# Layer 3: six of eight retrieved tiles turned in 32x32 squares and by transfers within SBUF, not by TensorE

## The chip, the cores and the metric

One core of a Trainium2 chip runs the whole program. The metric is device time in microseconds (us) of one execution, the median over several runs. All data is float32 unless a tile says otherwise.

## The reference

Four layers follow each other on x, which has 4 x 256 tokens of 512 features. Each layer normalises x and adds an attention part and a feed-forward part. Only the attention of layer 3 is touched here. It looks values up in a compressed memory:

```
q   = xn @ Wq.T + bq            # 8 heads of 128 (one per group of 4)
sig = elu(q) + 1
num = sig @ M[h]                # per head, 128 x 128
den = sig @ z[h] + 1e-6
retrieved = num / den           # per head, tokens x 128
out = repeat(retrieved, 4 heads) @ Wo.T
```

Since each retrieved head is used for four heads of Wo, the kernel adds up those four blocks of Wo beforehand, so `out` is a product with 8 x 128 = 1024 rows of summed output weights.

## The kernel before

The tokens are eight tiles of 128. A half is four of them. Large products are done in blocks by a seven-product scheme (Strassen's in Winograd's form, `seven`, L1325), so a product needs sums of input blocks as well as the blocks: s1 = a21 + a22, s2 = s1 - a11, s3 = a11 - a21, s4 = a12 - s2 (`summed`, L1105). Each of the seven products is a task.

The instructions of TensorE, VectorE, ScalarE and GpSimd are issued in the order in which the program writes them (`manual_schedule`, L1286). SyncE issues the transfers. Work is placed with `run(tasks)`, `after(k, f)` and `spread(k, steps)`: `after` puts f behind the task that comes k tasks later. Each engine works through its own list in that order and waits at an instruction whose inputs or buffer aren't ready.

The output of TensorE goes to eight PSUM banks with one buffer each (tags S, U, T, V, X, Y, Z, W). A bank must be read out by VectorE or ScalarE before TensorE can use it again.

Around the change, tile t = 0 to 7 goes through these steps:

- `retrieved(t)`, L1728: sixteen matmuls in three banks S, U, V (`num`, L1736, 129 columns per head, the last one the denominator). Then VectorE makes `den` (L1750) and its reciprocal (L1752), and ScalarE scales the eight heads into `ret` in SBUF (L1758, eight instructions). `ret` has three buffers.
- `turned(t, j, tag)`, L1765: four heads at a time, j = 0 and 1, are transposed by TensorE with the identity (`retT`, L1770, four instructions) into bank T (or Y) and copied by VectorE into a quarter of the half's input blocks (`rt_a`, L1776). Features must lie on the partitions, as the next product sums over them.
- `turned_sums(half)`, L1778: the four block sums on VectorE, 128 x 1024 elements each (`rt_s`, L1111, and L1115).
- `output_tasks` of the half: seven products of sixteen matmuls each with the summed weights (`wos_b`, `wos_t`; L1413).

Tiles 0 to 3 are half 0. Their steps are laid between the fourteen products of the second half's queries (L1377): `num` of tile t stands behind the (2t + 1)th of them, the two turnings behind the next two. Between those products VectorE also reads out query banks (`u`, `c`, `m` at L1349, L1357, L1367) and makes elu(q) + 1 from `e` and `sig` (L1694, L1700). The sums of half 0 are spread behind the tenth to thirteenth of the fourteen. Tiles 4 to 7 are half 1 and are laid between the output products of half 0, the sums of half 1 behind its last one. Then the output products of half 1 end the program.

Layer 2 has a step of the same kind as the change. It turns its probabilities in 32 x 32 squares on VectorE (L1853, `blocks<-p`) and moves the squares to their partitions by four transfers (L1858, `q<-blocks`).

Of the kernel before, what the change touches and what calls it, by code (L numbers as in the profile page):

```python
# [21 lines left out]
F32 = mybir.dt.float32  # L22
# [4 lines left out]
AF = mybir.ActivationFunctionType  # L27
ALU = mybir.AluOpType
# [3 lines left out]
P = 128  # L32
B, T, C = 4, 256, 512
# [18 lines left out]
L3_HEADS, L3_G = 8, 4  # L52
# [4 lines left out]
def block_stack(ctx: ExitStack, tc: tile.TileContext, d: dict, out: bass.AP):  # L57
    nc = tc.nc
# [13 lines left out]
    def ps(tag, shape, name):  # L72
        return banks["pool"].tile(shape, F32, tag=tag, name=name, bufs=banks["tags"][tag])
# [34 lines left out]
    for t in range(2):  # L108
# [3 lines left out]
    ident = const.tile([P, P], F32, name="ident")  # L112
# [7 lines left out]
        out=by_four,  # L120
        in_=by_four,
# [1141 lines left out]
    def layers_2_and_3(w, late):  # L1263
# [8 lines left out]
        with ExitStack() as stack:  # L1272
# [36 lines left out]
            A = w.A  # L1309
# [11 lines left out]
            def after(k, *fs):  # L1321

                due.setdefault(slot[0] + k, []).extend(fs)
# [199 lines left out]
            class Layer3:  # L1523
# [204 lines left out]
                def retrieved(self, t):  # L1728

                    half, i, tt = t // 4, t % 4 // 2, t % 2  # L1730
                    banks = []
                    for tag, h0, n in (("S", 0, 3), ("U", 3, 3), ("V", 6, 2)):
                        b = ps(tag, [P, n, ME], f"num_{t}_{h0}")
                        for k in range(n):
                            j, s, e = (h0 + k) // 4, (h0 + k) % 4 // 2, (h0 + k) % 2
                            nc.tensor.matmul(  # L1736
                                b[:, k, :],
                                lhsT=self.sig[half, s, (i, j)][:, e, tt * P : (tt + 1) * P],
                                rhs=self.mz[:, h0 + k, :],
                                start=True,  # L1740
                                stop=True,
                            )
                        banks.append((b, n))
                    ret = self.rets[t] = []

                    def divided():
                        den = small.tile([P, L3_HEADS], F32, tag="den", name=f"den_{t}")
                        for b, n in banks:
                            h = slice(len(ret), len(ret) + n)
                            nc.vector.tensor_scalar(den[:, h], b[:, :, P], 1e-6, None, ALU.add)  # L1750
                            ret.extend([None] * n)
                        nc.vector.reciprocal(den, den)  # L1752
                        r = self.late.tile([P, L3_HEADS, P], F32, tag="ret", name=f"ret_{t}", bufs=3)
                        h = 0
                        for b, n in banks:
                            for k in range(n):
                                ret[h] = r[:, h, :]
                                nc.scalar.activation(  # L1758
                                    ret[h], b[:, k, 0:P], AF.Copy, scale=den[:, h : h + 1]
                                )  # L1760
                                h += 1

                    after(0, divided)

                def turned(self, t, j, tag):  # L1765
                    half, i, tt = t // 4, t % 4 // 2, t % 2
                    A = self.retrieval[half]
                    tp = ps(tag, [P, 4, P], f"retT_{t}_{j}")
                    for k in range(4):
                        nc.tensor.transpose(tp[:, k, :], self.rets[t][4 * j + k], ident)  # L1770
                    key = f"a{i + 1}{j + 1}"
                    if key not in A:
                        A[key] = self.rt[half].tile(
                            [P, 4, T], F32, tag="rt", name=f"rt_{half}_{key}", bufs=7
                        )
                    nc.vector.tensor_copy(A[key][:, :, tt * P : (tt + 1) * P], tp)  # L1776

                def turned_sums(self, half):  # L1778
                    def make(k):
# [266 lines left out]
            l3 = Layer3()  # L2046
            for quad in range(QUADS - 1):
                gp, r = divmod(quad, 4)
# [22 lines left out]
                else:  # L2071
# [15 lines left out]
                    elif quad % 2 == 0 and quad < QUADS - 2:  # L2087

                        k = quad // 2
# [48 lines left out]
            for t in range(4):  # L2138
                k = len(tasks) + 2 * t
                after(k, lambda t=t: l3.retrieved(t))  # L2140
                for j in range(2):
                    after(k + 1 + j, lambda t=t, j=j: l3.turned(t, j, "T"))
            spread(len(tasks) + 9, l3.turned_sums(0))
            spread(len(tasks) + 6, [lambda t=t: l3.biased(t) for t in range(NT)])
            tasks += l3.query_tasks(1, 0) + l3.query_tasks(1, 1)
# [4 lines left out]
            for i, t in enumerate(range(4, NT)):  # L2150
                after(2 + i, lambda t=t: after(0, lambda: l3.retrieved(t)))
                for j in range(2):
                    after(3 + i, lambda t=t, j=j: l3.turned(t, j, "TY"[j]))
            after(6, lambda: [f() for f in l3.turned_sums(1)])
            run(tasks)
            run(output_tasks(l3.retrieval[1], l3.outputs, 1, fresh=True, last=True))
# [107 lines left out]
def _arrays(i):  # L2264
    c, j, r = np.meshgrid(np.arange(4), np.arange(8), np.arange(16), indexing="ij")
    order0 = (P * c + 8 * r + j).reshape(4, P)
    a = dict(_constants())
    a["x"] = i["L0_attn_x"].reshape(B * T, C)
    for n in ("wq", "wk", "wv"):
        a[n] = _chunked(i["L0_attn_" + n].T, order0)  # L2270
    a["wo"] = _chunked(i["L0_attn_wo"].T)

    def padded(w, axis, n):

        shape = list(w.shape)
        shape[axis] = n - shape[axis]
        return np.concatenate([w, np.zeros(shape, w.dtype)], axis)


    scales, zeros = [], []  # L2280
    for m in ("gate", "up"):
        q = padded(i[f"L0_ffn_{m}_qweight"], 1, NBLK * P).reshape(4, 16, NBLK, 16, 8)
        a[m + "_q"] = q.transpose(1, 2, 0, 4, 3).reshape(16, NBLK, 4, P)
        s = padded(i[f"L0_ffn_{m}_scales"], 1, NBLK * P).reshape(4, NBLK, 16, 8)
        scales.append(s.transpose(3, 2, 1, 0).reshape(P, NBLK, 4))
        zeros.append(padded(i[f"L0_ffn_{m}_zeros"], 1, ROWS).reshape(4 * NBLK, 16))
    a["gu_s"] = np.stack(scales, 1)
    a["gu_z"] = np.concatenate(zeros)
    q = padded(i["L0_ffn_down_qweight"], 0, ROWS).reshape(NBLK, 16, C)
    a["down_q"] = q.transpose(1, 0, 2)  # L2290
    a["down_s"] = i["L0_ffn_down_scales"]
    a["down_z"] = i["L0_ffn_down_zeros"]

    a["w1"] = _chunked(i["L1_ffn_W"].T)
    a["rank"] = _chunked(np.concatenate([i["L1_ffn_A"], i["L1_ffn_gate_w"]]).T)
    a["b1_rank"] = i["L1_ffn_B"].T
    a["b1_bias"] = i["L1_ffn_b"][None]
    a["gate_b"] = i["L1_ffn_gate_b"]
    a["bqk"] = np.stack([i["L1_attn_bv_q"].T, i["L1_attn_bv_k"].T], 1)
    a["bv"] = i["L1_attn_bv_v"]  # L2300

    wqkv = i["L2_attn_Wqkv"].T.reshape(2, 2, P, 48, P)
    nq = L2_GROUPS * L2_QH
    q = wqkv[:, :, :, :nq].reshape(2, 2, P, 4, 2, 2, 2, P)
    q = q.transpose(3, 5, 0, 4, 2, 1, 6, 7)
    kv = wqkv[:, :, :, nq:].reshape(2, 2, P, 2, 4, 2, P)
    kv = kv.transpose(4, 0, 5, 2, 1, 3, 6)
    a["wq2"] = q.reshape(8, 4, P, 2, 2 * P)  # L2310
    a["wkv2"] = kv.reshape(4, 4, P, 2, 2 * P)
    wo = i["L2_attn_Wo"].T.reshape(4, 2, 2, 2, P, 2, 2 * P)
    a["wo2"] = wo.transpose(0, 2, 1, 5, 4, 3, 6).reshape(8, 4, P, 2, 2 * P)
    w2 = i["L2_ffn_W_base"].T.reshape(2, 2, P, 2, 2 * P)
    a["w2"] = w2.transpose(0, 3, 2, 1, 4).reshape(1, 4, P, 2, 2 * P)
    ar = np.concatenate([i["L2_ffn_A_w"], i["L2_ffn_router_w"]]).T
    a["ar"] = _chunked(np.pad(ar, ((0, 0), (0, 32 - ar.shape[1]))))
    a["cores"] = i["L2_ffn_cores"].reshape(EXPERTS * RANK, RANK).T
    a["bw"] = i["L2_ffn_B_w"].T
    a["b2"] = i["L2_ffn_b_base"]  # L2320

    m, k, q = np.meshgrid(np.arange(2), np.arange(2), np.arange(P), indexing="ij")
    order3 = (2 * P * m + 2 * q + k).reshape(NC, P)
    wq3 = i["L3_attn_Wq"].reshape(L3_HEADS, L3_G, P, C)[:, 0].reshape(L3_HEADS * P, C)
    w = wq3.T[order3.reshape(-1)].reshape(2, 2, P, 2, 2, 2, P)
    a["wq3"] = w.transpose(4, 0, 3, 2, 1, 5, 6).reshape(2, 4, P, 2, 2 * P)
    a["bq3"] = i["L3_attn_bq"].reshape(L3_HEADS, L3_G, P)[:, 0].T
    a["wo3"] = i["L3_attn_Wo"].T.reshape(L3_HEADS, L3_G, P, C).transpose(0, 2, 1, 3)
    a["mz"] = np.concatenate([i["L3_attn_M"], i["L3_attn_z"][:, :, None]], -1).transpose(1, 0, 2)
    a["pk3"] = _chunked(i["L3_ffn_weight_packed"].reshape(C, C // 2).T)  # L2330
    a["scale3"] = i["L3_ffn_scale"][:, 0]
    a["zero3"] = i["L3_ffn_zero_point"][:, 0]
    a["b3"] = i["L3_ffn_bias"]
    return {k: np.ascontiguousarray(v) for k, v in a.items()}
# [17 lines left out]
```

## Time and profile before

| | us |
|---|---|
| median of three runs (1354.12 to 1357.17) | 1356.17 |
| the profiled execution | 1355.85 |
| its span on the core | 1354.1 |
| TensorE busy | 1306.8 |
| VectorE busy | 930.0 |
| layer 3 from its first `num` to the end of the span | 1253.3 to 1354.1 |

The profiled execution took 1.75 us more than its span. Times in a trace are us from the start of the span. The granted TensorE clock was 0.995 of full speed over the run. A matmul's recorded end is modelled and lies behind the start of the next one, so for TensorE the distance from start to start counts, which is what the chain of waits shows.

### The profile page before, as it was taken

The numbers are of one execution on the slowest core, as the hardware profiler recorded it, in microseconds if no ns is written. First come the engines' busy times: TensorE is split into PE (matmuls) and PEld (weight loads), VectorE is DVE, ScalarE is ACT, GpSimd is POOL, SyncE is SP. The second block draws the span as 40 slices with busy tenths as digits, with TensorE's granted clock in tenths as the row PEclk, the third lists the DMA queues.
The fourth block names the chain that finished last, engine by engine and source line by source line (L and its number), as shares of the span: only waits on it lengthen the run. The fifth ranks groups of instructions, "written<-read, shape, count | busy, mean of one in ns | idle before, by whom it ended". The sixth has DMA issues, their size and how long they took to land. (4 is left out here: it accounts for less than half of the span.)

```text
span 1354.1 us, 20458 instructions
## 1 busy us (share of the span) xinstructions
PE 1306.8 (97%) x7076; PEld 1024.0 (76%) x7076; DVE 930.0 (69%) x1969; ACT 561.7 (41%) x1474; POOL 658.1 (49%) x662
## 2 busy tenths in 40 slices
PE   9899999899998998999999999999999999899998
PEld 7566666588545667888888888888888888677887
DVE  7676667478927249846867968777678776668654
ACT  2444434388212213423443443444434454555530
POOL 4555456477746104663576745757356563021410
PEclk9999999999999999999999999999999999999999
DMA  5022222400610021331333424433334333413001
GB/s 203 14 48 43 41 48 68 101 1 0 175 66 8 0 85 40 83 82 51 113 114 94 124 63 122 116 94 101 81 87 125 90 78 83 144 24 117 1 1 62
DMA packets 92792, 101.44 MB, mean 75 GB/s; under 512 B 21147, under 2 KB 65846, under 8 KB 92305
## 3 DMA queue, kind: packets, MB, share of 16 engines
q1 hardware_dynamic: 91760, 99.08, 26.4%
q8 instruction: 56, 0.92, 0.3%
q10 hardware_dynamic: 816, 0.79, 0.2%
q14 instruction: 48, 0.39, 0.1%
q0 software_dynamic: 112, 0.26, 0.1%
HBM read 67.02 MB, written 7.91 MB: 55 GB/s over the span
## 5 line engine op out<-in xcount | busy, mean ns | idle before, releaser
L1830 ACT ACTIVATE p<-p,nm 128x256 f32<-128x256 f32 (+1 forms) x256 | 113.2, 443 | 158.1 <-DVE nm L1814 157.3
L1427 POOL TENSOR_TENSOR q<-q,t 128x512 f32<-128x512 f32 x64 | 82.0, 1281 | 130.1 <-DVE t L1432 128.3
L1845 ACT ACTIVATE p<-p,rs 128x256 f32<-128x256 f32 (+1 forms) x256 | 95.5, 444 | 39.9 <-DVE rs L1841 39.9
L1377 PE MATMUL m<-xT,wq_b 128*128 128x256 f32 x448 | 103.9, 380 | 2.1 <-ACT kv L1483 2.0
L1432 DVE TENSOR_TENSOR t<-m,rope_sb 64x512 f32<-64x512 f32 (+1 forms) x144 | 95.3, 662 | 1.9
L1377 PEld LDWEIGHTS m<-xT,wq_b 128*128 128x128 f32 x448 | 82.4, 190 | 12.7 <-ACT kv L1483 2.4
L1360 POOL TENSOR_TENSOR c<-c,z 128x512 f32<-128x512 f32 x28 | 36.5, 1303 | 112.8 <-DVE c L1357 54.5
L1853 DVE STREAM_TRANSPOSE blocks<-p 128x768 f32<-128x768 f32 x64 | 62.6, 978 | 41.1 <-ACT p L1845 39.4
L1413 PE MATMUL m<-wo_b,o 128*128 128x256 f32 x384 | 89.6, 379 | 0.0
L1881 ACT COPY o<-av 128x512 f32<-128x512 f32 x64 | 37.3, 583 | 118.2 <-PE av L1871 115.8
L1814 DVE CUSTOM_DVE_ANT_0 p<-s,cmask 128x256 f32<-128x256 f32 (+1 forms) x256 | 76.1, 353 | 12.9 <-PE s L1795 11.2
L475 POOL TENSOR_SCALAR_AFFINE_SELECT keys<-keys 128x256 f32<-128x256 f32 x128 | 56.7, 453 | 49.9 <-ACT keys L471 43.6
L1492 DVE TENSOR_TENSOR x_sb<-x_sb,m 128x512 f32<-128x512 f32 x82 | 54.9, 679 | 36.6 <-PE m L1413 25.3
L1413 PEld LDWEIGHTS m<-wo_b,o 128*128 128x128 f32 x384 | 71.9, 190 | 9.2
L757 PE MATMUL dn<-wd,hT 128*128 128x512 f32 x176 | 76.4, 593 | 0.7 <-ACT o L753 0.7
L814 POOL TENSOR_TENSOR sa<-sa,sb 128x1024 f32<-128x1024 f32 x22 | 62.2, 2830 | 30.6 <-DVE sb L809 30.6
L1377 PE MATMUL m<-x_s,wq_t 128*128 128x256 f32 x320 | 74.1, 380 | 2.4 <-ACT kv L1483 2.0
L471 ACT ACTIVATE keys<-st 128x384 f32<-128x384 f32 x128 | 55.9, 487 | 38.9 <-PE st L461 38.9
L1870 PE MATMUL av<-q,kv 128*128 128x512 f32 x128 | 66.5, 601 | 3.9 <-DMA q<-blocks 3.9
L1377 PEld LDWEIGHTS m<-x_s,wq_t 128*128 128x128 f32 x320 | 60.2, 190 | 12.1 <-ACT kv L1483 2.4
L1795 PE MATMUL s<-kv,q 128*128 128x256 f32 x256 | 65.9, 380 | 0.4 <-POOL q L1427 0.4
L757 PEld LDWEIGHTS dn<-wd,hT 128*128 128x128 f32 x176 | 33.2, 190 | 41.1 <-issue 39.5
(328 smaller groups left out, 3283.8 us busy)
## 6 DMA issues: line engine op xcount, KB each, us to landing
q<-blocks SPq DMA_DIRECT2D x256, 96.0 KB, 2.3
wq_b<-in_wq SPq DMA_DIRECT2D x38, 256.0 KB, 2.8
wo_b<-in_wo SPq DMA_DIRECT2D x32, 256.0 KB, 2.8
raw<-in_wo SPq DMA_DIRECT2D x24, 256.0 KB, 3.2
wkv_b<-in_wkv SPq DMA_DIRECT2D x16, 256.0 KB, 2.8
wos_d<-wos_row SPq DMA_DIRECT2D x28, 128.0 KB, 3.3
gate_q<-in_gate_q SPq DMA_DIRECT2D x11, 256.0 KB
up_q<-in_up_q SPq DMA_DIRECT2D x11, 256.0 KB
```

The costliest lines, as they stand in the source:

```text
L757: nc.tensor.matmul(po, lhsT=hT[:, k, t * P : (t + 1) * P], rhs=wd[:, k, :], start=k == 0, stop=k == NBLK - 1,)
L814: nc.gpsimd.tensor_tensor(self.a, self.a, self.b, ALU.add)
L1377: nc.tensor.matmul(out[:, i, :], lhsT=b[:, c, i * P : (i + 1) * P], rhs=a[:, c, :], start=start and i == 0 and c == 0, stop=i == 1 and c == 1,
L1413: nc.tensor.matmul(out[:, t, :], lhsT=a[:, c, t * P : (t + 1) * P], rhs=b[:, c, :], start=start and t == 0 and c == 0, stop=t == 1 and c = ...
L1427: after(1 + 2 * pause, lambda: nc.gpsimd.tensor_tensor(dst, dst, t2, ALU.add))
L1432: nc.vector.tensor_tensor(t2[at], src[of], sin[of], ALU.mult)
L1795: nc.tensor.matmul(s1[:, i, :], lhsT=q[:, i, P:T], rhs=kt[:, 0, :], start=True, stop=True)
L1814: nc.vector.tensor_tensor_reduce(out=x[f"p{part}"][:, e, :], in0=x[f"s{part}"][:, e, :], in1=cmask if part else cmask[:, P : 2 * P], scale ...
L1830: nc.scalar.activation(p, p, AF.Exp, bias=x["nm"][:, part, e : e + 1], scale=-1.0, accum_out=x["sums"][:, part, e : e + 1],)
L1845: nc.scalar.activation(p, p, AF.Copy, scale=x["rs"][:, part, e : e + 1])
L1853: nc.vector.transpose(blocks, x["p"].rearrange("p e x (b i) -> p b (e x) i", b=4))
L1870: nc.tensor.matmul(av, lhsT=v[:, 0:P], rhs=q[:, :, :, 0:64], start=True, stop=False)
```

## The change

For tiles 0 to 5, TensorE no longer transposes. VectorE turns the four heads of a `turned` step in one instruction, in 32 x 32 squares, from `ret` into a tile `blocks` in SBUF that has two buffers, so that the turning of tile t + 1 waits until the transfers of the same j of tile t have landed. Then SyncE issues four transfers, one for each group of 32 partitions, that move the squares from SBUF to SBUF into the quarter `A[key]`. A transfer is 64 KB, from 32 partitions to 128, in pieces of 32 elements, which is 128 B. The PSUM copy (`rt_a`) falls away with the transposes.

By this path feature 32 b + i comes to lie on partition 4 i + b, where TensorE's transpose leaves feature f on partition f. So the weights Wo are laid out in the same order on the host (`wo3`), and for tiles 6 and 7, which TensorE still turns, ScalarE writes `ret` in that order. `ret` has two buffers instead of three.

```diff
-                        r = self.late.tile([P, L3_HEADS, P], F32, tag="ret", name=f"ret_{t}", bufs=3)
+                        r = self.late.tile([P, L3_HEADS, P], F32, tag="ret", name=f"ret_{t}", bufs=2)
+                        self.rets[t] = r
...
-                                ret[h] = r[:, h, :]
-                                nc.scalar.activation(
-                                    ret[h], b[:, k, 0:P], AF.Copy, scale=den[:, h : h + 1]
-                                )
+                                dst, src = r[:, h, :], b[:, k, 0:P]
+                                if t >= 6:
+                                    dst = dst.rearrange("p (i b) -> p b i", b=4)
+                                    src = src.rearrange("p (b i) -> p b i", b=4)
+                                nc.scalar.activation(dst, src, AF.Copy, scale=den[:, h : h + 1])
...
-                def turned(self, t, j, tag):
+                def turned(self, t, j):
                     half, i, tt = t // 4, t % 4 // 2, t % 2
                     A = self.retrieval[half]
-                    tp = ps(tag, [P, 4, P], f"retT_{t}_{j}")
-                    for k in range(4):
-                        nc.tensor.transpose(tp[:, k, :], self.rets[t][4 * j + k], ident)
+                    ret = self.rets[t][:, 4 * j : 4 * j + 4, :]
...
-                    nc.vector.tensor_copy(A[key][:, :, tt * P : (tt + 1) * P], tp)
+                    if t >= 6:
+                        tp = ps("TY"[j], [P, 4, P], f"retT_{t}_{j}")
+                        for k in range(4):
+                            nc.tensor.transpose(tp[:, k, :], ret[:, k, :], ident)
+                        nc.vector.tensor_copy(A[key][:, :, tt * P : (tt + 1) * P], tp)
+                        return
+                    b = self.late.tile([P, 4, 4, 32], F32, tag="blocks", name=f"blocks_{t}_{j}", bufs=2)
+                    nc.vector.transpose(b, ret.rearrange("p k (b i) -> p b k i", b=4))
+                    for a in range(4):
+                        n = tt * P + 32 * a
+                        nc.sync.dma_start(out=A[key][:, :, n : n + 32], in_=b[32 * a : 32 * a + 32])
...
-    a["wo3"] = i["L3_attn_Wo"].T.reshape(L3_HEADS, L3_G, P, C).transpose(0, 2, 1, 3)
+    wo3 = i["L3_attn_Wo"].T.reshape(L3_HEADS, L3_G, 4, 32, C)
+    a["wo3"] = wo3.transpose(0, 3, 2, 1, 4).reshape(L3_HEADS, P, L3_G, C)
```

TensorE's list loses twelve groups of four transposes, SyncE's gains twelve groups of four transfers, and VectorE's keeps its order and length, with a turning in squares wherever a copy out of PSUM stood. The stores of the output come behind the new transfers on SyncE, in the order of before.

## The prediction

> **What bounds the kernel now.** TensorE is busy for 1306.8 of 1354.1 us, so a gain must come out of TensorE's list or its waits. The chain of waits for the stage, cut where it repeats, shows which engine ends last:
>
> ```profile
> 1271.25 0.44 PE retT L1770 x4
> 1271.69 1.73 PE m L1377 x8
> 1273.42 0.44 PE retT L1770 x4
> 1273.86 1.79 PE num L1736 x16
> 1275.64 1.73 PE m L1377 x8
> 1277.37 0.45 PE retT L1770 x4
> ...
> 1281.03 0.67 DVE e L1694 x2
> 1281.70 1.13 DVE rt_s L1111
> 1282.83 1.20 DVE sig L1700 x2
> ...
> 1287.84 0.61 DVE c L1357
> 1288.45 0.04 issue
> 1288.50 1.99 PE m L1377 x8
> ```
>
> From 1258 to 1278 TensorE is the chain, and a group of four transposes costs 0.44 us of it. From then to 1288.5 VectorE is. Busy times by stage (columns: stretch, length, then PE, PEld, DVE, ACT, POOL busy, clock, DMA share, GB/s) say the same, and that no transfers run here:
>
> ```profile
> 1266.00:1272.00 6.00, 6.00 (x42) 5.49 (x41) 2.44 (x8) 2.54 (x10) 2.80 (x3) 1.00 0.00 1
> ...
> 1278.00:1290.00 12.00, 10.92 (x51) 8.77 (x50) 12.00 (x17) 6.15 (x15) 2.69 (x3) 1.00 0.00 0
> ...
> 1300.00:1326.00 26.00, 26.00 (x167) 23.76 (x167) 11.06 (x31) 9.18 (x33) 0.00 (x0) 1.00 0.01 2
> ```
>
> VectorE has 12.00 of 12.00 us to do while half 0's sums are made. Whatever delays the first sum (s1, 1281.62 in the timeline) delays TensorE at 1288.50 one for one.
>
> The price of the new path is read from the same step in layer 2, from the view of its tile `blocks`:
>
> ```profile
> L1858 SPq DMA_DIRECT2D q<-blocks x256: 542/602/1510, 543.1 to 1205.2; - x128
> L1853 DVE STREAM_TRANSPOSE blocks<-p x64: 966/978/980, 542.1 to 1202.3; 128x768 f32<-128x768 f32 x64
> ...
> DMA to landing us min/median/max: 2.3/2.3/4.4
> ```
>
> In SyncE's timeline, four of these issues take 2.59 us, 0.65 each.
>
> **Removed.** Tiles 0 to 3: eight groups x 0.44 = 3.5 us of TensorE, and the 1.40 us that it waits at 1258.35 for the first `ret`. Tiles 4 and 5: two pieces of the chain, 0.87 and 1.14, so 2.0 us, in a stretch where TensorE is never idle. Taken alone that is 6.9 us. The PSUM copies stood off the chain but for the last.
>
> **Added on VectorE.** Twelve turnings of 128x512. At 978 ns for 768 columns one is between 0.65 (in proportion) and 0.98 us; the copy that it replaces took 0.69. I take 0.70, so nothing. What changes is what it waits for: four `ret` instructions (0.27 us each) and, from tile 1 on, the landing of the four transfers of the tile before. Behind it on VectorE stand `den`, without which no `ret` comes, and the bank readings `u`, `c`, `m`, for which TensorE waits.
>
> **Added on SyncE.** 48 issues. Tiles 0 to 3 have 32 of them, 32 x 0.65 = 20.8 us, one after the other from about 1259.8. The nearest other row in spacing is two 512-piece transfers (`gate_z`, `up_z`), issued at 64.45 and 64.96, 0.51 us apart. Bounds 0.51 and 0.65; I take 0.65, since `q<-blocks` also goes from 32 partitions to 128. Nothing is queued behind these transfers but the output stores, first issued at 1331.93.
>
> **Added on the DMA engines.** A transfer is 64 KB in 512 pieces of 128 B. No row has such pieces. The nearest are 512 pieces of 256 B (`up_z`, 128 KB) and 128 of 768 B (`q<-blocks`, 96 KB), in two stretches that hold little else:
>
> ```profile
> 88.00:88.40 0.40, 0.40 (x16) 0.13 (x4) 0.40 (x2) 0.28 (x1) 0.40 (x1) 1.00 0.98 184
> ...
> 544.40:546.90 2.50, 2.50 (x17) 2.32 (x16) 2.37 (x5) 0.00 (x0) 2.32 (x2) 1.00 0.69 148
> ```
>
> By count of pieces a transfer occupies the engines as long as `up_z` does: 128 KB / 184 GB/s = 0.71 us. By bytes at 148 GB/s it is 0.44. Both lie near the 0.65 between issues, so I let the issue set the pace; the upper end I put at 1.0 us, since the 512 pieces of `gate_z`, beside a 256 KB transfer, ended only after the 2.1 us from 80.0 to 82.1. Landing: `q<-blocks` has 2.3 us, the low end; `gate_z`, as many pieces, has 4.3 at least, the high end, but behind that 256 KB transfer, which at 184 GB/s is 1.4 us of it. I take 4.3 - 1.4 = 2.9, the row with as many pieces.
>
> Here a rule speaks against the change. The Trainium skill, DMA: Bandwidth & Descriptors, Specifications, gives 512 B as the least transfer for line rate, smaller ones being read, modified and written. Taken so that a 128 B piece costs what a 512 B one does, it makes an estimate of 1.8 us a transfer and some 37 us on the sum. The same page, Why small descriptors are slow (HBM only), exempts transfers from SBUF to SBUF, which would leave 0.44 us and this forecast. The 256 B pieces above ran at 184 GB/s at a share of 0.98, the 768 B ones at 148 / 0.69 = 214, which is nearer to the second; no run here shows 128 B.
>
> **The sum.** With spacing 0.65 and landing 2.9, step by step (B = turning, D = last of its four transfers landed):
>
> - Tile 0: `ret` begins at 1257.93 as now, its fourth ends 1259.0. B00 1259.1 to 1259.8; four issues from 1259.8, the last at 1261.75, D00 1264.65. B01 1260.4 to 1261.1, issues from 1262.4, D01 1267.25.
> - Tile 1: without transposes `num` ends at 1260.95 instead of 1263.24, `ret` begins at 1262.3 instead of 1263.94. But B10 waits for D00, to 1265.4, and B11 for D01, to 1268.0. D10 1270.25, D11 1272.85.
> - Tile 2: `c` 1268.0, `den` 1268.6, `ret` 1269.2 (now 1270.05). B20 to 1271.05, B21 waits for D11, to 1273.6. D20 1275.9, D21 1278.5.
> - Tile 3: `m`, `e`, `den`, `ret` 1275.25 (now 1276.25). B30 to 1277.1, B31 to 1279.25. Issues for B30 from 1277.1, for B31 from 1279.7, D31 1284.55.
>
> So TensorE is up to 4 us ahead at tile 2, and VectorE takes it back: s1 needs tile 3's transfers and begins at 1284.6 instead of 1281.62. Before, its input came by a PSUM copy that ended 0.6 us earlier; now VectorE stands idle from about 1279.9 to 1284.6. The 6.8 us of VectorE from s1 to TensorE's wait at 1288.50 have no gap to make it up, so 3.0 us are lost there, in place of the 4.9 us gained.
>
> In the last stage 1.8 of the 2.0 us remain: tile 4's transfers land about 1313 and tile 5's by 1321 before the shift, while TensorE reads that quarter first at 1325.4; 0.2 is for `ret` of tile 6, whose `den` now stands behind two turnings. Tiles 6 and 7 with their strided `ret`: nothing (a copy of that kind, `o<-av`, takes 583 ns for 512 columns against 590 for plain ones).
>
> Sum: +3.0 - 1.8 = +1.2 us. On the profiled 1355.85 that is 1357.05, on the median 1356.17 it is 1357.4. About 0.2% (2.7 us) is what a measurement of this kernel tells from no change, so this is no change that can be told. Landing 2.3 instead of 2.9 gives s1 at 1283.1, so -0.3; the count-bound pace of 0.71 gives s1 at about 1286.2 and +3 us. This case alone holds -0.5 to +3: 1355.7 to 1359.2.
>
> **Rivals.**
>
> 1. *The transfers land late, slower.* The ring of two ties tile t + 1 to tile t. If landing is 4.0, a tile lasts 0.7 + 3 x 0.65 + 4.0 = 6.65 us against TensorE's 5.25 (2 x 1.73 + 1.79): s1 at 1288, +6.5, of which the last stage gives back 1.5, so +5. It decides from a landing of about 3.3 us on. For it: four times the pieces. Against: 2.3 is steady over 256 transfers.
> 2. *The engines set the pace, slower by more.* At 1.0 us a transfer the 32 take 32 us, s1 begins near 1259.8 + 32 + 1.9 = 1293.7, +12. It begins above 0.71 us. For it: a source of 32 partitions and the smallest pieces yet. Against: 0.44 by bytes.
> 3. *SyncE issues faster, faster kernel.* With 0.51 and 2.3 the same list gives D00 1263.6, D11 1270.3, D21 1275.35, D31 1280.5: s1 1.1 us earlier than now, -1.1 - 1.8 = -2.9. For it: 0.51 between transfers of as many pieces. Against: 0.65 wherever 32 partitions go to 128.
>
> **How the numbers follow.** Forecast case 0.40, of which 0.32 within 0.2% and 0.08 slower; rival 1 0.26; rival 2 0.12; rival 3 with anything better 0.22. So faster 0.22, same 0.32, slower 0.46: the likeliest single case lies within 0.2%, though the slower ones together hold more. The range runs from 1352.9 (rival 3 and 0.4 below) to 1368.0 (rival 2 at 1.0 us).
>
> **What would show it.** Right: SyncE issues 0.65 us apart without pause in the stage, B10, B11 and B21 idle before a DMA, and VectorE idle for 4 to 5 us before the first `rt_s`, at 1284 to 1285. Wrong: spacing under 0.55 or landings over 3.3, `rt_s` before 1282 or after 1287, or TensorE waiting between the output products of half 0 (1290 to 1326), where I see no new wait.

## The result and the profile after

| kernel | median, us | lowest to highest | runs |
|---|---|---|---|
| before | 1354.35 | 1350.39 to 1357.17 | 12 |
| after | 1358.01 | 1356.05 to 1360.73 | 12 |

The ratio after to before is 1.0030, with a 95% interval from 1.0018 to 1.0042. So the change makes the kernel slower by some 4 us. The median lies within the predicted range and 0.6 us above the predicted time. Part of that nearness is owed to the kernel before, whose median was 1.8 us lower here than in the three runs that the prediction started from: the difference is +3.7 us where +1.2 was forecast. The measured 0.30% lies outside the likeliest case, within 0.2%, though the lower end of the interval, 0.18%, touches it.

The profiled execution of after took 1356.17 us with a span of 1354.5, hardly more than that of before. Its work ahead of the change happened to run 3.9 us earlier: the first `den` of tile 0 is at 1253.39 in its timeline and at 1257.31 in that of before. All that the change touches lies behind this instruction, so below every time is counted from the first `den`.

| from the first `den`, us | before | after | difference |
|---|---|---|---|
| first sum (s1, `rt_s`) | 24.31 | 28.31 | +4.00 |
| first output product of half 0 | 33.02 | 38.17 | +5.15 |
| first output product of half 1 | 68.11 | 72.34 | +4.23 |
| end of the span (known to 0.1) | 96.8 | 101.1 | +4.3 |

The loss arises before half 0's output products, and a piece of it comes back in the last stage. The chain of waits of after shows where (start us, us, what):

```profile
1270.32 1.02 DVE e L1694
...
1273.06 0.71 DVE blocks L1784
1273.77 0.84 DVE sig L1700
...
1275.98 0.70 DVE blocks L1784
...
1277.36 1.02 SPq L1787
...
1279.10 2.43 DMA rt_a<-blocks
...
1281.70 1.23 DVE rt_s L1111
...
1286.32 5.41 PE m L1377 x16
...
1317.80 1.97 PE retT L1780 x8
```

Where `retT` and products carried the chain before, it now goes through VectorE's `e`, `sig` and turnings, SyncE's queue (SPq) and the landing of the last transfer to s1. From there it goes on through VectorE to TensorE's products at 1286.32. The windows of after, with the columns of before:

```profile
1266.00:1272.00 6.00, 6.00 (x36) 5.17 (x34) 3.43 (x8) 2.81 (x10) 6.00 (x6) 1.00 0.66 90
1272.00:1278.00 6.00, 2.38 (x9) 2.03 (x9) 4.26 (x6) 5.48 (x17) 2.90 (x3) 0.90 0.59 81
1278.00:1290.00 12.00, 8.45 (x27) 6.66 (x27) 8.30 (x11) 2.30 (x5) 1.32 (x1) 0.78 0.17 22
```

VectorE, busy for all 12.00 us of the third window before (and for 11.30 us of 1281.92 to 1293.92, the stretch that lies as far behind the first `den`), now works 8.30 of them. TensorE is busy for 2.38 of the 6 us from 1272, and the granted clock falls to 0.90 and 0.78, where it was 1.00 before. The view of the tile `blocks` prices the new path:

```profile
L1787 SPq DMA_DIRECT2D rt_a<-blocks x48: 609/634/1342, 1255.9 to 1317.4; - x48
L1784 DVE STREAM_TRANSPOSE blocks<-ret x12: 695/711/712, 1255.2 to 1314.5; 128x512 f32<-128x512 f32 x12
...
  DMA rt_a<-blocks: 9.1, 5
...
  DVE rt_s L1111: 4.4, 1
```

and the DMA view of after from 1253 to 1284 gives the landing of half 0's 32 transfers, in the median:

```profile
rt_a<-blocks SPq DMA_DIRECT2D x32, 64.0 KB, 2.5
```

VectorE waited 9.1 us for transfers ahead of five turnings and 4.4 us ahead of s1. In the trace the issues stand mostly 0.68 us apart, and the usual landing, from the start of an issue, is 2.45 us.

The clock is a new item. TensorE's timeline of after (in brackets: idle time before, and what ended it):

```profile
1275.63 2.71 PE L1377 MATMUL m<-x_s,wq_t 128*128 128x256 f32 x8 [3.62 <-ACT sig L1688]
...
1286.32 3.14 PE L1377 MATMUL m<-x_s,wq_b 128*128 128x256 f32 x8 [3.55 <-ACT z L1352]
1289.25 2.48 PE L1377 MATMUL m<-xT,wq_t 128*128 128x256 f32 x8
```

Eight such products stand 1.73 us from start to start at full clock. From 1286.32 they take 2.93 and then 2.31 us (1291.56, the first output product, less 1289.25). The trace's clock records have half speed for 3.41 us from 1276.77 and again from 1287.01, each behind an idle time of over 3.5 us. Before, no half speed is recorded between 1253 and 1350.

### The profile page after: what moved, and what is told of

The parts are those of the page before. It is cut to its first block, busy times and chain, and to the rows that moved or that the text cites. A ratio compares the mean times of both kernels' runs of the same rounds, so it can differ in the third digit from the quotient of the medians.

```text
span 1354.5 us, 20478 instructions
## 1 busy us (share of the span) xinstructions
PE 1303.2 (96%) x7028; PEld 1023.0 (76%) x7028; DVE 931.0 (69%) x1969; ACT 561.8 (41%) x1474; POOL 657.2 (49%) x662
```

## The experiments

The theory: half 0's sums stand in VectorE's fixed order, and the new path brings their input about 4 us too late. The late transfers also let TensorE fall idle, which costs clock. The rivals: the loss comes from the last stage, from the ring of two buffers alone, from the DMA engines, or from the clock alone. Each run was also timed against the kernel before; "ratio" is against that. Times are from the first `den`, in us.

| run | s1 | first output product | end of span | ratio (95% interval) |
|---|---|---|---|---|
| before | 24.31 | 33.02 | 96.8 | 1 |
| after | 28.31 | 38.17 | 101.1 | 1.0030 (1.0018 to 1.0042) |
| e1_tail_only | 24.42 | 33.13 | 95.4 | 0.9988 (0.9976 to 1.0000) |
| e2_head_only | 28.56 | 39.54 | 103.5 | 1.0043 (1.0029 to 1.0058) |
| e3_late_sums | 29.30 | 33.60 | 96.4 | 0.9985 (0.9970 to 1.0000) |
| e8_before_late_sums | 29.22 | 32.07 | 95.9 | 0.9995 (0.9983 to 1.0006) |
| e9_tail_late | 31.03 | 33.88 | 96.1 | 0.9989 (0.9977 to 1.0000) |
| e5_four_blocks | 27.42 | 38.18 | 100.0 | 1.0016 (1.0002 to 1.0029) |
| e6_two_queues | 27.47 | 36.19 | 98.0 | 1.0017 (1.0004 to 1.0030) |
| e12_both | 27.41 | 36.12 | 97.9 | 1.0019 (1.0006 to 1.0032) |
| e7_filled | 27.78 | 38.61 | 102.2 | 1.0031 (1.0017 to 1.0046) |
| e11_filled_half | 27.86 | 37.78 | 100.0 | 1.0011 (0.9997 to 1.0024) |
| e13_pool_later | 27.65 | 38.76 | 101.0 | 1.0042 (1.0026 to 1.0059) |
| e10_two_queues_late | 30.01 | 32.85 | 95.1 | 0.9981 (0.9969 to 0.9993) |

An interval is some 3 us wide. The times tell the slow group (1.003 to 1.004) from the fast one (0.998 to 1.000). The intervals of the middle group (1.001 to 1.002) overlap that of after, so there, and within a group, only the traces can tell, and they are of one execution each.

### The two halves of the change (e1_tail_only, e2_head_only)

In the first, only tiles 4 and 5 go the new way, in the second only tiles 0 to 3; the other tiles use TensorE as before.

```diff
-                                if t >= 6:
+                                if t not in (4, 5):
...
-                    if t >= 6:
-                        tp = ps("TY"[j], [P, 4, P], f"retT_{t}_{j}")
+                    if t not in (4, 5):
+                        tp = ps("T" if t < 4 else "TY"[j], [P, 4, P], f"retT_{t}_{j}")
```

> Only tiles 4 and 5 are turned by VectorE and moved by transfers; tiles 0 to 3, 6 and 7 by TensorE. Queue theory (the loss of the changed kernel lies in half 0, where 32 transfers pass one queue before the first block sum): half 0 is as before, s1 starts as long after the first den as before (24.3 us), no half-speed clock in the stage, and the last stage keeps what four transpose groups cost: 0.9 to 2.0 us less than the kernel before. Rival (small transfers cost wherever they stand, VectorE's waits eat the gain): no gain or a loss, 0 to +2 us.

> Only tiles 0 to 3 by the new path, tiles 4 to 7 by TensorE. Queue theory: the whole loss of half 0 without the gain of the last stage: s1 about 28.3 us after the first den (24.3 before), the half-speed clock as in the changed kernel, +5 us on the kernel before, 1 to 2 us above the changed kernel. Rival (the loss is spread over both halves): +2 to +3 us.

Measured: 0.9988 and 1.0043. The two effects, -0.12% and +0.43%, add up to the +0.30% of the change, rounding aside. So the last stage gains about 1.5 us, though the interval of e1 reaches to 1.0000, and half 0 loses nearly 6. With tiles 0 to 3 on TensorE, s1 is back at 24.42.

### Half 0's sums later (e3_late_sums, e8_before_late_sums)

The same edit in after (e3) and in before (e8):

```diff
-            spread(len(tasks) + 9, l3.turned_sums(0))
+            spread(len(tasks) + 12, l3.turned_sums(0))
```

> The changed kernel with the four block sums of half 0 placed three tasks later (spread behind tasks 14 to 17 after the second half's queries begin, not 10 to 13). In-order theory (VectorE stands 4.4 us at the first sum for the last landing, with query readings behind it): that wait falls under 1 us, the output products begin 4 to 5 us earlier than in the changed kernel, 3 to 5 us less in all, so 0 to 1.5 us below the kernel before. Rival (the transfers' ring holds VectorE back anyway, at the turnings): the wait only moves, less than 1.5 us regained.

> The kernel before with its block sums of half 0 placed three tasks later, the control for the other run. If VectorE's full stretch from 1278 to 1290 is what TensorE waits for there (0.25 + 1.19 + 0.68 us), it gains 1 to 2 us on the kernel before. If the sums then delay the output products, it gains nothing.

Measured: 0.9985 and 0.9995, so the edit takes 0.45% (6 us by the times, 4.7 us by the traces) off the change and hardly anything off the kernel before. VectorE's timeline of e3:

```profile
1279.74 0.69 DVE L1784 STREAM_TRANSPOSE blocks<-ret 128x512 f32<-128x512 f32 x1
...
1286.49 1.22 DVE L1111 TENSOR_TENSOR rt_s<-rt_a,rt_a 128x1024 f32<-128x1024 f32 x1
```

Between the two VectorE makes the query work that was queued behind s1, and s1 waits for nothing (no bracket). The last transfer lands 28.2 us after `den`, later than the 28.1 of after; yet the output products begin at 33.60, not 38.17. So what cost time was not that the transfers were late, but that an instruction waiting for them stood in VectorE's order ahead of work that TensorE needed. This is the clearest of the runs.

### Tail alone with later sums (e9_tail_late)

e1_tail_only with the edit of e3.

> VectorE and transfers for tiles 4 and 5 alone, TensorE for tiles 0 to 3 and 6 and 7, and half 0's sums three places later. Theory (the last stage's gain of 1.4 to 1.6 us is there for the taking and the later sums cost nothing): 1.5 to 3 us faster than the kernel before, the best so far. Rival (the later sums push half 0's output products back without the early turning): as the kernel before, within 1 us.

Measured: 0.9989, 1.5 us faster, the lower edge of what was expected, and no better than e1_tail_only without the edit. The rival, within 1 us of before, lies inside the interval too. The trace can't decide, for it has 3.41 us of half speed from 1255.74, where no other trace has any: TensorE's eight products at 1255.52 last 3.19 us there instead of 1.73, and s1 and the first output product, at 31.03 and 33.88, each come 1.81 us later than in e8.

### Four buffers (e5_four_blocks)

The squares of j = 1 go into another pool's two buffers, so each j has a ring of its own.

```diff
-                    b = self.late.tile([P, 4, 4, 32], F32, tag="blocks", name=f"blocks_{t}_{j}", bufs=2)
+                    if j:
+                        b = lnp.tile([P, C], F32, tag="xn", name=f"blocks_{t}_{j}")
+                        b = b.rearrange("p (b k i) -> p b k i", b=4, k=4)
+                    else:
+                        b = self.late.tile([P, 4, 4, 32], F32, tag="blocks", name=f"blocks_{t}_{j}", bufs=2)
```

> The change with a ring of two buffers for each j, so four for the turned squares instead of two. Theory (the sums stand in order behind 32 issues of 0.68 us): the 9.1 us of VectorE's waits for transfers go, but the queue stays: 24 issues are through 18.9 us after the first den, tile 3's values come about then, and 8 more issues and a landing of 2.4 us put the first sum at 26.9 instead of 28.3; with what the freed VectorE brings the gates forward 1.5 to 2.5 us of the 4.3 are regained. Rival A (the two-buffer ring is the whole cost): all 4 us come back, the first sum at 24.3. Rival B (neither the ring nor the queue, only the landing of the last transfer): nothing, within 0.5 us of the change.

Measured: 1.0016, s1 at 27.42. From the view of its tile `blocks`, waits ahead of turnings and ahead of s1:

```profile
  DMA rt_a<-blocks: 1.3, 1
...
  DVE rt_s L1111: 7.7, 1
```

Of the 9.1 us of waits ahead of turnings 1.3 remain, and the wait ahead of s1 grows from 4.4 to 7.7. The 32 issues now stand without a pause from 2.53 to 24.82 us after `den`, and the last lands at 27.24. So with the ring out of the way the queue alone keeps s1 at 27.4: that part of the theory holds, and the ring is worth 0.9 us of s1. The longer stop of VectorE left TensorE idle for 8.10 us, with half clock for 10.24, so the first output product came no earlier than in after. What the trace regains by its end, 1.1 us, comes from the last stage, which the theory did not name: no turning of tile 5 waits for a transfer there, and tile 6's transposes take their old 0.87 us in the chain instead of 1.97.

```profile
1316.90 0.87 PE retT L1780 x8
```

### Two queues (e6_two_queues, e12_both)

e6 is after with half of the issues on ScalarE's queue, e12 the same with the four buffers of e5.

```diff
-                        nc.sync.dma_start(out=A[key][:, :, n : n + 32], in_=b[32 * a : 32 * a + 32])
+                        (nc.scalar if a > 1 else nc.sync).dma_start(out=A[key][:, :, n : n + 32], in_=b[32 * a : 32 * a + 32])
```

> The change with the third and fourth transfer of each group issued by ScalarE instead of SyncE. Theory (the issues set the pace): a group passes in 1.4 us instead of 2.7, the last lands about 24 us after the first den, the first sum runs on time at 24.3, and 3 to 5 us come back. Rival A (the 16 DMA engines set the pace, busy 0.70 now): landing stretches over 3.5 us and under 1 us comes back. Rival B (ScalarE pays): its 16 issues of some 0.6 us delay ret and sig, the gates come late, and at most 2 us come back.

> e5_four_blocks and e6_two_queues together: four buffers, and half of the transfers issued by ScalarE. Theory (once the ring no longer holds the turnings and the queue has half the issues, nothing else is late): the last transfer lands before 24.3 us after the first den, the first sum runs on time, VectorE waits for no transfer, and 3 to 4 us of the 4.3 come back. Rival (16 issues take ScalarE 10 us, which ret and sig wait for): the first sum at 26 to 27.5 as in e5_four_blocks and e6_two_queues alone, and under 2.5 us come back.

Measured: 1.0017 and 1.0019, with s1 at 27.47 and 27.41. My theory falls in both: halving the queue did not bring s1 to 24.3. The signs of both rivals of e6 are there. From the view of e12's tile `blocks`, who waited for a turning:

```profile
  ACT ret L1761: 3.3, 1
  ACT acc L1502: 2.6, 1
  ACT u L1347: 1.5, 1
```

ScalarE works in order too: its issues wait for the turning and then take about 0.68 us each (median of 24: 675 ns), and `u`, `ret` and, in the last stage, `acc` stand behind them. Tile 3's first turning begins 18.56 us after `den` in e12, and 15.91 in e5. That is rival B. With two issues at a time the landings grew too, in the median to 3.9 us (SyncE) and 3.4 (ScalarE) in e6, and the last, of 4.31 us, is what s1 waits for. While both queues issued, the DMA engines were busy for 0.97 of the time at 138 GB/s (e12, 1264 to 1267), where one queue had kept them busy for 0.71. That is rival A: a second queue meets the limit of the engines. How much each rival took was not separated. Still both traces show the output products 2 us earlier than after. Only 0.84 us of that is s1 in e6, and the rest is the clock. In e6's TensorE timeline:

```profile
1286.22 1.99 PE L1377 MATMUL m<-x_s,wq_b 128*128 128x256 f32 x8 [1.85 <-ACT z L1352]
1288.49 1.99 PE L1377 MATMUL m<-xT,wq_t 128*128 128x256 f32 x8 [0.28 <-DVE c L1357]
1290.33 3.62 PE L1413 MATMUL m<-wos_b,rt_a 128*128 128x256 f32 x16
```

The same group began at 1286.32 in after, and s1 at 1281.61 here and at 1281.70 there. At full clock the first output product comes 8.72 us behind s1, as in before (8.71), against 9.86 in after. So half clock cost after 1.1 us. The other traces agree. From s1 to the first output product it is 8.71 us where no half speed falls between them (before, e1, e12), 9.86 and 9.92 with 3.41 us of it (after, e11), and 10.98 and 11.11 with 6.83 us (e2, e13).

### TensorE kept busy (e7_filled, e11_filled_half)

Spare products, 26 or 13 at each of two places, that nobody reads:

```diff
+            def filled(k, n):
+                def f():
+                    x = ps("T", [P, P], "fill")
+                    for _ in range(n):
+                        nc.tensor.matmul(x, lhsT=ident, rhs=ident, start=True, stop=True)
+
+                after(k, f)
+
+            filled(19, 26)
+            filled(22, 26)
```

> The change with 26 spare products of the identity (2.9 us at full clock) put in TensorE's order where it sat idle 3.6 us, twice; they are read by nobody. Theory (the two stretches at half clock cost 1.2 us beside the late sums): the clock stays full, eight products take 1.73 us again instead of 2.3 to 2.9, the first sum stays at 28.3, and about 1 us comes back. Rival A (TensorE waits for the sums whatever its clock): nothing, within 0.4 us. Rival B (the spare products stand in front of real ones): 1 to 3 us slower still.

> As e7_filled, but 13 spare products at each place: in e7_filled's trace 26 of them held TensorE 5.8 us, 2.2 us longer than the idle time that they were to fill, so half of them hold it 2.9 us. Theory (the half clock costs 1.2 us): the clock stays full, no real product waits for a spare one, the output products begin about 37 us after the first den instead of 38.2, and about 1 us comes back. Rival (the clock hides behind the late sums): they begin at 38, and nothing comes back, within 0.4 us.

Measured: 1.0031 and 1.0011. In e7 the clock stays full and the real groups stand 1.73 us apart, but the 26 spare products are 52 instructions and hold TensorE 5.8 us instead of the 2.9 that I had allowed. They stood in front of real ones, which is its rival B, though of its 1 to 3 us more than after only 1.1 show in the trace and none in the ratio. With the clock full s1 still came at 27.78, so the clock alone is not the loss. In e11 the first half-speed stretch is gone and the second is not:

```profile
1287.92 2.51 PE L1377 MATMUL m<-x_s,wq_b 128*128 128x256 f32 x8 [2.00 <-ACT z L1352]
```

Its first output product comes at 37.78 instead of 38.17, and 9.92 us behind s1, as with half clock. The ratio points to a gain over after, but the intervals overlap. As a test of the 1.1 us the pair is inconclusive; e6 is the better one.

### GpSimd's block later (e13_pool_later)

```diff
-            spread(len(tasks) + 6, [lambda t=t: l3.biased(t) for t in range(NT)])
+            spread(len(tasks) + 14, [lambda t=t: l3.biased(t) for t in range(NT)])
```

> The change with GpSimd's block of eight additions to x_sb (8.8 us, in the stage of tiles 2 and 3) put eight places later, behind half 0's sums. Theory (VectorE's e and sig, 1.11 and 1.75 us in the change's trace, are long because GpSimd works beside them): they take about 0.4 and 0.7, the last turning ends about 1.5 us earlier after the first den than the 23.3 of the change, the first sum begins at about 27 instead of 28.3, and 1 us or a little more comes back. Rival A (they are long of themselves): still 1.1 and 1.75, the first sum at 28.3, nothing comes back. Rival B (the block slows what it now lies beside): the first sum at 27, but the products begin no earlier than 38, within 0.4 us of the change or slower.

Measured: 1.0042. VectorE's timeline:

```profile
1273.50 0.41 DVE L1694 TENSOR_SCALAR e<-sig 128x512 f32<-128x512 f32 x1
...
1276.27 0.65 DVE L1700 SCALAR_TENSOR_TENSOR sig<-sig,e 128x512 f32<-128x512 f32 x1
...
1284.46 1.23 DVE L1111 TENSOR_TENSOR rt_s<-rt_a,rt_a 128x1024 f32<-128x1024 f32 x1 [5.07 <-DMA rt_a<-blocks]
```

`e` took 0.41 instead of 1.11 us and `sig` 0.65 instead of 1.75: the theory of the slowdown holds. Tile 3's second turning begins at 21.23 after `den` instead of 22.59. But of these 1.36 us s1 gets 0.66, the rest goes in one issue of 1.31 us, and nothing reaches the products. The outcome is rival B's, its cause is not: the block starts at 1293.52, when the last group before the products is under way. TensorE begins the group before that, at 1289.08, as far behind s1 as in after (4.62 us), but now 6.83 us of half speed follow, from 1288.22, where after has 3.41, and the two groups take 6.49 us instead of 5.24:

```profile
1289.08 3.78 PE L1377 MATMUL m<-x_s,wq_b 128*128 128x256 f32 x8 [3.86 <-ACT z L1352]
```

So the clock takes 1.25 us, more than the 0.66 that s1 had gained. The block, which now lies beside the first output products, takes 11.94 us for eight additions (8.81 for seven in after), and two of VectorE's `sig` there take 2.55.

### Two queues and later sums (e10_two_queues_late)

The edits of e6 and e3 together.

> e6_two_queues with half 0's sums three places later, as in e3_late_sums. Theory (late sums already take the queue's lateness off the path, so that a shorter queue finds nothing left): as e3_late_sums, 1 to 2.5 us faster than the kernel before, within 1 us of e3_late_sums. Rival (the queue still costs beside late sums, by the products' start 0.6 us later than before): 1 us or more faster than e3_late_sums.

Measured: 0.9981 (0.9969 to 0.9993), about 2.6 us faster than before, and the only run whose interval lies wholly below 1. Its products begin at 32.85. It is the best version found; that it beats e3_late_sums, as its trace says by 1.2 us at the end of the span, the times do not show. In the stage of half 0, e3's trace has 6.83 us of half speed and e10's none, so a part of the 1.2 us can be that, and not the queue.

## Why the prediction was right or wrong

**The mechanism was right, its size was not.** The new wait is where the text put it: s1 waits for tile 3's transfers, TensorE's 4.9 us are taken back by VectorE, and s1 to the products has no slack. e3 shows it from the other side. Counted from `den`, the list of steps holds up to tile 2: B11 begins at 10.05 (forecast 9.99) and B21 at 15.63 (15.59). Of the signs that were named, B11 and B21 waited for transfers and VectorE stood idle for 4.4 us ahead of s1; B10 waited for `ret` and not for a transfer; s1, at 1285.6 in the time of before, lies between the sign of being right (1284 to 1285) and that of being wrong (after 1287); and TensorE did wait between the output products, at tile 6's transposes, which was named as a sign of being wrong.

**Spacing and landing** were each a little off and cancelled: 0.68 instead of 0.65 in 32 issues, 2.45 instead of 2.9 in each landing. In a steady stretch, 1258 to 1266, the DMA engines were busy for 0.71 of the time at 96 GB/s, so a 64 KB transfer occupied them 0.48 us (0.68 x 0.71), near the 0.44 by bytes and below the 0.71 by count. The issues set the pace, as forecast. Of the two statements on small transfers that the prediction weighed, the one with the estimate of 1.8 us a transfer does not hold for these 128 B pieces; the one that exempts SBUF to SBUF is much nearer. Small pieces are not free, though: while busy, the engines moved 96 / 0.71 = 135 GB/s here, against the 214 that the prediction worked out for 768 B pieces.

**The step "B31 to 1279.25" was mis-sized.** In time from `den`, B31 should have begun at 21.24 and began at 22.59. `e` and `sig` of tile 3 ran on VectorE beside the 8.8 us of GpSimd's block of additions to x_sb, and took 1.8 us more than in e13. There, without the block, B31 begins at 21.23. The trace of before had the hint, `e` at 0.58 and `sig` at 1.38 us with the same block running, and I did not follow where it would fall. The Trainium skill says as much (SBUF — State Buffer, Who interferes with whom): a VectorE instruction with two inputs in SBUF contends with a GpSimd instruction that reads SBUF, one in a mode that uses both ports contends too, and one with a single input outside these modes does not. That agrees with `sig`, which has two inputs, and with the turnings, which have one and took 0.71 us with the block and without it. `e` has one as well; that it ran in such a mode no run shows.

**So s1 was 1.0 us later than forecast** (28.31 against 27.29): 1.35 from B31, less the shorter landing.

**The clock was missing from the sum.** "The 6.8 us of VectorE from s1 to TensorE's wait have no gap" was right for VectorE, but the list counted TensorE's products at full speed, and they ran at half: 1.1 us, by e6. The two idle times follow from the forecast itself, which had TensorE ahead and then waiting, and I put no price on them. The Trainium skill (TensorE: Matmul & The Clock Gate, What's actually happening) gives half speed after an idle window of about 3.4 us, in free-running windows of 3413 ns. The stretches of 3.413 us agree; that a whole window must be idle does not, since half speed followed idle times of 2.00 us (e11) and 1.52 us (e9) as well.

**The last stage gave 0.9 instead of 1.8 us.** The transposes of tile 6 hold the chain for 1.97 us instead of 0.87. The step allowed 0.2 for `ret` of tile 6 behind two turnings; these waited 1.56 and 2.12 us for tile 4's transfers. In e1 the first of them did not wait for a transfer, the second waited 1.79 us, and the chain piece was 1.34. So what the step had too small is the turnings' wait for the ring of two, which stands ahead of tile 6's `den`. From the first product of half 0 to that of half 1 the stage gained 2.0 us in e5, e6 and e12, where tile 6's transposes took 0.87 us; 1.53 to 1.59 in e1, e9, e10, e11 and e13, with the ring of two and no issue of tiles 4 and 5 above 1.0 us; and 0.92, 1.03 and 0.25 in after, e3 and e7, where one issue of tile 4 or 5 took 1.34, 1.19 and 1.51 us instead of 0.63.

The sum with measured terms, up to half 1's first product: 4.00 + 1.15 - 0.92 = +4.23.

**The rivals.** Rival 1 named nearly the right size, +5, by a ring that waits for landings of 4.0. The ring did make turnings wait, but the usual landing was 2.45, below the 3.3 from which rival 1 decides, so its price is refuted and its size was a coincidence. Rival 2 would need the engines busy all the time; they were busy 0.71. Rival 3 needed 0.51 between issues; they had 0.68. The chances, with 0.46 on slower, were better than the choice of the single likeliest case, which took every unseen interference at nothing.

## What to carry to other kernels

When work moves from a busy engine to a longer path, ask first which instruction waits for its end and what stands behind that on its in-order engine: here, moving four sums three places later was worth more than a larger ring or a second queue. Price what the earlier work will now run beside, and the clock of the engine that is left idle, as terms of the sum. A queue that moves to another engine takes that engine's order with it, and the waits as well.

## What the runs showed of the hardware that was not expected

Half speed comes in units of 3.413 us, and within one trace all its starts lie on one grid of that step: in after 1164.13, 1276.77 and 1287.01 are 33 and 3 steps apart. An idle time of 2.00 us was followed by half speed in e11; one of 2.85 us was not in e10:

```profile
1278.92 1.99 PE L1377 MATMUL m<-x_s,wq_t 128*128 128x256 f32 x8 [2.85 <-ACT sig L1688]
```

By the grid of its other stretches, the idle time in e10 fell across two windows and that in e11 within one. e1 and e9, alike up to here, had the same idle time ahead of tile 0's transposes, 1.54 and 1.52 us. It fell across two windows in e1 and within one in e9, and only e9 has half speed behind it. That is not the whole rule either: in e12 1.9 of 2.18 us fell within one window, and no half speed followed. The runs give no single length from which it happens. So a trace of one execution can hold such a loss by where its windows fall, in e9 1.8 us.

Single issues of SyncE took 1.0 to 1.6 us instead of 0.63 us, as at 1277.36 in after. Each of them (in after, e2, e3, e5, e7, e11, e12 and e13) has a transfer of instructions of 16 KB running beside it, which in after begins at 1277.06 and, for the issue of 1.34 us in the last stage, at 1308.38. The DMA view of after from 1276 to 1282 shows the first (packets, MB, share of 16 engines):

```profile
q1 hardware_dynamic: 3584, 0.44, 55.1%
q8 instruction: 1, 0.02, 0.9%
```

Where the profile has the landing of such an issue, it was 2.8 us (after, 1277.36) and 3.1 us (e13) instead of 2.45. The reverse does not hold: in e13 an instruction transfer at 1310.35 ran beside issues of 0.61 and 0.63 us. No run took these transfers away, so that they cause the delay is only argued. They fall at other places in each kernel, and with the ring of two the last stage gained least where an issue was long (0.92 us in after, against 1.53 to 1.59 in the five runs above without one).
